# Four cross-attention and FFN layers: query projection by pairs of groups with a DMA spread, work moved to GpSimd, and a source order on two more engines

## The chip, the cores and the metric

The kernel runs on one core of a Trainium2 chip. The metric is the device time of one execution in microseconds. Before the change three runs gave a median of 4570.16 us (4563.57 to 4571.57). A separate profiled execution took 4577.85 us; the profile's span, from its first to its last instruction, is 4576.1 us. PE is the tensor engine, DVE the vector engine, ACT the scalar engine, POOL is GpSimd and SP the queue that issues most DMAs.

## The reference, cut to what matters

The input is `x` of 2048 rows by 256, a context of 1601 rows by 192 and a mask over the context. Four layers follow one another. Each adds a cross-attention of the normalised rows to the context, and then an FFN of the normalised rows.

```python
x = x + xattn(_layernorm(x), ctx)      # layers 0, 1, 3: 16 heads of 16; layer 2: 8 heads of 32
x = x + ffn(_layernorm(x))

# xattn
q, k, v = x @ wq + bq, ctx @ wk + bk, ctx @ wv + bv
scores = q k^T / sqrt(d)               # layer 3: masked context columns get -max
out = softmax(scores) v @ wo + bo

# ffn, with a router on the same normalised rows
# layer 0: sigmoid scores, 2 of 4 groups, then 4 of 16 experts, plus a shared MLP
# layer 1: 2 of 8 experts, gelu MLP of 1024;  layer 2: 2 of 8 linear experts
# layer 3: 2 of 16 experts with a capacity of 320 rows, plus a shared MLP and the row itself
```

Everything is computed in float32.

## The kernel before, in words

The rows are held in SBUF as four blocks of 512 rows (`x[b]`, each four tiles of 128 rows). The context is held transposed as `ctxT` (192 rows, and one further row of ones that carries the biases). Heads are worked on in four groups of 128 partitions: four heads in layers 0, 1, 3 (32 partitions for each, of which the head's 16 and two helpers are used), two in layer 2.

`load_attention` loads a layer's weights. It scatters the query weights on POOL into a padded copy `wq` of 512 columns, so that a projected group comes out already spread over its partitions. In layer 3 it also loads the mask as one row `mrow`. `keys_values` projects the keys in 16 tiles of about 400 columns, two matmuls each (lines 227 and 230), and in layer 3 a third matmul with one row of input (line 235) that writes the mask into a helper row of the keys. It then projects the values in 13 tiles.

`attention` then works in 16 steps, one for each block and group. A step has three parts.

- Maxima: `project_queries` (line 263, and the copy with bias and scale on ACT, line 267) makes `q1`. `max_unit` computes a score tile of 128 rows by 512 keys and reduces it to row maxima on DVE (lines 276, 283); `max_tails` does the last 65 keys (lines 292, 300). `max_rows` puts the maxima into a padded tile `mp`, and `with_maxima` transposes it and adds it to `q1` (lines 319, 320), so that the later exponential needs no subtraction.
- Scores: `score` computes transposed score tiles of 128 keys by 512 rows (line 328) and ACT takes the exponential (lines 336, 338).
- Values: `values` accumulates them over 13 key tiles (line 346). `copy_out` copies the accumulator (line 502), `normalise` transposes and divides (lines 358 to 362). After the four groups of a block, `outputs_T` and `project` add the projected output to `x[b]` (lines 374, 383, 391).

The order of this work is written out. `ORDER` lists one period of tokens, M for a maximum, S for a score, P for the values of a key tile; a step's maxima stand beside the scores and values of the step before it. Two slots make a period, and a step is 13 slots long. An agenda (`at(slot, ...)`) places the rest at slots: `points` are the slots two after the last maxima of a step. A query projection is placed two points ahead of its end in layers 0, 1, 3 (one in layer 2), the normalisation `rows(b)` for a block's queries four slots ahead of its transposes. After a block's output projection, `after(b)` gives the FFN's normalisation `rows`, its transposes `rows_T` and the router `route`. `norm_rows` (lines 398 to 406) takes the statistics, the power of -1/2 (on POOL, line 403) and the scaling on DVE, in one go.

In the loop's main part the tensor engine keeps this written order (`tc.manual_schedule` with `EngineType.PE`). On all other engines, and outside of that part, the framework's scheduler decides the order when the program is built. The first slots of a layer (its lead, maxima only) are issued in pieces between the FFN work of the layer before, and there too only PE's order is fixed. PSUM tiles come from one ring of seven banks, which maxima, scores, transposes and projections share; a bank comes free when DVE or ACT has read it.

Of the kernel before, what the change touches and what calls it, by code (L numbers as in the profile page):

```python
# [11 lines left out]
F32 = mybir.dt.float32  # L12
I32 = mybir.dt.int32
U32 = mybir.dt.uint32
U8 = mybir.dt.uint8
# [4 lines left out]
P = 128  # L20
# [4 lines left out]
NB = 4  # L25
# [41 lines left out]
def block_stack(ctx: ExitStack, tc: tile.TileContext, I: dict, out: bass.AP):  # L67
# [28 lines left out]
    nc.vector.memset(ctxT[DC - P : DC - P + 1, 1, :], 1.0)  # L96
    C1, C2 = P, DC - P + 1
# [24 lines left out]
    nc.vector.memset(neg_half, -0.5)  # L122

# [4 lines left out]
    nc.vector.tensor_scalar(mcol, mcol8, -1.0, BIG, ALU.add, ALU.mult)  # L128


    def load_attention(L):
# [3 lines left out]
        wq_raw = wp.tile([P, 2, D], F32, tag="wq_raw", name=f"wq_raw{n}")  # L135
        nc.sync.dma_start(wq_raw, I[f"wq{n}"])
        wq = wp.tile([P, 2, H * S], F32, tag="wq", name=f"wq{n}")
        nc.gpsimd.memset(wq, 0.0)
        wqv = wq.rearrange("p c (h s) -> p c h s", s=S)
        wqr = wq_raw.rearrange("p c (h e) -> p c h e", e=d)  # L140
        for g in range(NG):
            hs, up = slice(g * J, (g + 1) * J), L.up[g]
            nc.gpsimd.tensor_copy(wqv[:, :, hs, up : up + d], wqr[:, :, hs])
        W["q"] = wq
        kw = 2 * D if L.fused else D
        wk_raw = wp.tile([P, 2, kw], F32, tag="wk_raw", name=f"wk_raw{n}")
        nc.sync.dma_start(wk_raw[:, 0, :], I[f"wk{n}"][0:P, :])
        nc.sync.dma_start(wk_raw[0 : DC - P, 1, :], I[f"wk{n}"][P:DC, :])
        if L.biased:
            nc.sync.dma_start(wk_raw[DC - P : C2, 1, :], I[f"bk{n}"])  # L150
        else:
            nc.vector.memset(wk_raw[DC - P : C2, 1, :], 0.0)
# [3 lines left out]
        else:  # L156
            wv_raw = wp.tile([P, 2, D], F32, tag="wv_raw", name=f"wv_raw{n}")
            nc.sync.dma_start(wv_raw[:, 0, :], I[f"wv{n}"][0:P, :])
            nc.sync.dma_start(wv_raw[0 : DC - P, 1, :], I[f"wv{n}"][P:DC, :])
            if L.biased:  # L160
                nc.sync.dma_start(wv_raw[DC - P : C2, 1, :], I[f"bv{n}"])
            else:
                nc.vector.memset(wv_raw[DC - P : C2, 1, :], 0.0)
            k_src = wk_raw.rearrange("p c (h e) -> p c h e", e=d)
# [6 lines left out]
        nc.gpsimd.memset(wk[DC - P : C2, 1, :], -1.0)  # L171
        wkv = wk.rearrange("p c (h s) -> p c h s", s=S)
        for g in range(NG):
            hs, up = slice(g * J, (g + 1) * J), L.up[g]
            nc.gpsimd.tensor_copy(wkv[:, 0, hs, up : up + d], k_src[:, 0, hs])
            nc.gpsimd.tensor_copy(wkv[0:C2, 1, hs, up : up + d], k_src[0:C2, 1, hs])
        W["k"] = wk
        if L.masked:
            mk = wp.tile([1, J, S], F32, tag="mk", name=f"mk{n}")
            nc.vector.memset(mk, 0.0)  # L180
            nc.vector.memset(mk[:, :, d + 1 : d + 2], 1.0)
            mrow8 = wp.tile([1, M], U8, tag="wB", bufs=2, name="mrow8")
            nc.sync.dma_start(mrow8, I["mask_row"])
            mrow = wp.tile([1, M], F32, tag="wA", bufs=2, name="mrow")
            nc.vector.tensor_scalar(mrow, mrow8, -1.0, BIG, ALU.add, ALU.mult)
            W["mk"], W["mrow"] = mk, mrow
        bq = wp.tile([P, NG], F32, tag="bq", name=f"bq{n}")
        nc.vector.memset(bq, 0.0)
        if L.biased:
            for j in range(J):  # L190
                if J == 4:
                    nc.sync.dma_start(bq[j * S : j * S + d, :], I[f"bq{n}"][j])
                else:
                    for g in range(NG):
                        at = j * S + L.up[g]
                        nc.sync.dma_start(bq[at : at + d, g : g + 1], I[f"bq{n}"][j, :, g : g + 1])
        if L.masked:

            row = small.tile([P, 1], F32, tag="row", name="row")
            nc.vector.tensor_reduce(  # L200
                row, ident.rearrange("p (j s) -> p s j", s=S)[:, d + 1, :], AX.X, ALU.add
            )
            nc.vector.tensor_copy(bq, row.to_broadcast([P, NG]))
        else:
            nc.vector.tensor_scalar(bq, bq, L.scale, None, ALU.mult)
        W["bq"] = bq
# [11 lines left out]
    def keys_values(L, W):  # L218
# [4 lines left out]
        for g in range(NG):  # L223
            for lo, hi in zip(KEYB[:-1], KEYB[1:]):
# [7 lines left out]
                    start=False, stop=not L.masked,  # L232
                )
                if L.masked:
                    nc.tensor.matmul(
                        o, W["mk"].rearrange("o j s -> o (j s)"), W["mrow"][:, lo:hi], start=False, stop=True
                    )
# [21 lines left out]
    def project_queries(L, W, xnT, g):  # L259

        pq = ps_misc()
        for c in range(2):
            nc.tensor.matmul(  # L263
                pq, W["q"][:, c, g * P : (g + 1) * P], xnT[:, c, :], start=(c == 0), stop=(c == 1)
            )
        q1 = act.tile([P, BT], F32, tag="q", bufs=5, name="q1")
        nc.scalar.activation(q1, pq, AF.Identity, bias=W["bq"][:, g : g + 1], scale=L.scale)  # L267
        mx = small.tile([P, NT, L.J, len(KB) - 1], F32, tag="mx", name="mx")
        return q1, mx
# [34 lines left out]
    def max_rows(L, mx, g):  # L304

        d, S = L.d, L.S
        mp = act.tile([P, NT, P], F32, tag="mp", name="mp")
# [1215 lines left out]
```

## Time and profile before

| what | value |
|---|---|
| median of three runs | 4570.16 us (4563.57 to 4571.57) |
| profiled execution, its own time | 4577.85 us |
| span in its profile | 4576.1 us |
| mean granted PE clock | 0.952 |
| busy: PE, DVE, ACT, POOL | 4377.1, 2459.4, 1984.1, 436.9 us |
| maxima on DVE (line 283) | 2688 of 684 ns |
| exponentials on ACT (line 338, line 336 in layer 3) | 2080 of 599 ns, 832 of 686 ns |
| query projection on PE (line 263) | 256 records, 122.6 us |
| mask matmuls of layer 3 (line 235) | 32 records, 400-column ones 950 ns |
| scaling of the rows on DVE (line 406) | 128 of 406 ns |

The page cuts the span into 40 slices and gives each engine's busy share in tenths, and the granted clock of PE in tenths of full speed. Every float32 matmul appears as two records in the trace. A row of a group gives line, engine, operation, output and inputs, count, busy time, mean duration of one, and the idle time of the engine ahead of it with the engine that ended it. Matmuls overlap, so a group's mean is longer than the distance between two starts. A row of a timeline gives start, duration, engine, line, operation and count, and in brackets the idle time ahead of it and what ended it.

### The profile page before, as it was taken

What the parts mean: (1) busy time and instruction counts of PE and PEld (TensorE: products, weight loads), DVE (VectorE), ACT (ScalarE), POOL (GpSimd) and SP (SyncE); (2) the same over time, 40 slices, a digit from 0 to 9 for tenths busy, and PEclk for the clock granted to TensorE, in tenths of its full rate; (3) what the DMA queues carried; (4) which work ended last, traced back from release to release, by engine and by line L of the source; (5) the groups of instructions that cost most, each with busy time, mean ns of one, the idle gap of its engine ahead of it and who ended that gap; (6) DMA issues with size and microseconds to landing.
All of it is one profiled execution on the core that took longest, in us unless ns stands there. A gap on an engine that the chain in (4) does not pass through costs nothing. (4 is left out here: it accounts for less than half of the span.)

```text
span 4576.1 us, 62597 instructions
## 1 busy us (share of the span) xinstructions
PE 4377.1 (96%) x25260; PEld 2003.0 (44%) x25260; DVE 2459.4 (54%) x5215; ACT 1984.1 (43%) x3718; POOL 436.9 (10%) x515
## 2 busy tenths in 40 slices
PE   8999999999999999999997999999999999999795
PEld 5333333366643334336885333343443333333463
DVE  5666766424777666653223645441486667663222
ACT  1655655611156655563221344432016666665010
POOL 1000000000000000003444000000000000000323
PEclk8999999999999999999998899997799999999897
DMA  2000000000000000002542000000000000000054
GB/s 73 1 1 1 1 1 3 1 25 1 1 1 1 1 6 1 8 6 66 178 158 72 1 1 1 1 1 3 10 13 1 1 6 1 6 1 10 26 143 122
DMA packets 56952, 108.89 MB, mean 24 GB/s; under 512 B 16733, under 2 KB 38101, under 8 KB 52054
## 3 DMA queue, kind: packets, MB, share of 16 engines
q0 software_dynamic: 20864, 55.18, 4.2%
q1 hardware_dynamic: 35798, 49.71, 3.4%
q8 instruction: 199, 3.26, 0.3%
q14 instruction: 91, 0.75, 0.1%
HBM read 138.37 MB, written 16.88 MB: 34 GB/s over the span
## 5 line engine op out<-in xcount | busy, mean ns | idle before, releaser
L283 DVE TENSOR_REDUCE mx<-ps_m 128x1 f32<-128x512 f32 x2688 | 1701.0, 684 | 684.1 <-PE ps_m L276 398.5
L328 PE MATMUL ps_s<-q,kT 32*128 32x512 f32 (+2 forms) x5824 | 1741.1, 628 | 8.6 <-DVE mx L283 8.4
L276 PE MATMUL ps_m<-kT,q 32*128 32x512 f32 x5376 | 1601.8, 645 | 8.5 <-issue 6.0
L338 ACT ACTIVATE e<-ps_s 128x512 f32<-128x512 f32 (+1 forms) x2080 | 1112.3, 599 | 874.1 <-PE ps_s L328 685.6
L346 PE MATMUL ps_acc<-e,V 128*32 128x512 f32 (+2 forms) x5824 | 931.7, 612 | 5.7 <-ACT a L502 5.7
L328 PEld LDWEIGHTS ps_s<-q,kT 32*128 32x128 f32 (+2 forms) x5824 | 579.7, 182 | 691.9 <-DVE mx L283 406.9
L276 PEld LDWEIGHTS ps_m<-kT,q 32*128 32x128 f32 x5376 | 574.6, 188 | 487.8 <-issue 392.5
L336 ACT ACTIVATE e<-ps_s,mcol 128x512 f32<-128x512 f32 (+1 forms) x832 | 515.6, 686 | 238.0 <-PE ps_s L328 158.3
L346 PEld LDWEIGHTS ps_acc<-e,V 128*32 128x32 f32 (+2 forms) x5824 | 160.5, 112 | 644.0 <-issue 506.8
L309 POOL MEMSET mp<- 128x512 f32 x64 | 33.3, 527 | 2451.4 <-PE ps_m L319 2443.2
L1030 ACT ACTIVATE h<-ps_h,w 128x128 f32<-128x128 f32 x320 | 91.3, 369 | 218.1 <-issue 130.0
L267 ACT ACTIVATE q<-ps_m,bq 128x512 f32<-128x512 f32 x64 | 44.0, 688 | 295.4 <-PE ps_m L263 295.4
L809 DVE SCALAR_TENSOR_TENSOR x<-ps_m,cw,x 128x256 f32<-128x256 f32 x256 | 110.8, 479 | 92.6 <-PE ps_m L801 89.6
L1022 PE MATMUL ps_h<-xT,w 128*128 128x128 f32 x1280 | 152.7, 279 | 0.0
L772 ACT ACTIVATE h<-ps_h 128x512 f32<-128x512 f32 x80 | 47.7, 597 | 235.0 <-PE ps_h L771 235.0
L1022 PEld LDWEIGHTS ps_h<-xT,w 128*128 128x128 f32 x1280 | 149.4, 195 | 0.1
L300 DVE TENSOR_REDUCE mx<-ps_m 128x4 f32<-128x260 f32 x224 | 80.3, 422 | 126.0 <-PE ps_m L292 126.0
L1044 PE MATMUL ps_m<-w,h 128*128 128x256 f32 x640 | 144.6, 379 | 0.0
L361 DVE RECIPROCAL rec<-ps_m 128x16 f32<-128x16 f32 (+1 forms) x64 | 15.4, 240 | 206.9 <-PE ps_m L358 206.9
L1044 PEld LDWEIGHTS ps_m<-w,h 128*128 128x128 f32 x640 | 118.6, 190 | 14.5
L263 PE MATMUL ps_m<-xnT,wq 128*128 128x512 f32 x256 | 122.6, 610 | 0.2 <-ACT xnT L417 0.2
L1267 DVE TENSOR_TENSOR h<-ps_h,sg 128x320 f32<-128x320 f32 (+3 forms) x60 | 31.8, 530 | 167.5 <-PE ps_h L1260 123.0
(266 smaller groups left out, 3306.0 us busy)
## 6 DMA issues: line engine op xcount, KB each, us to landing
gu<-in_w_gate SPq DMA_DIRECT2D x16, 352.0 KB
gu<-in_w_up SPq DMA_DIRECT2D x16, 352.0 KB
ys_dram<-ys SPq DMA_DIRECT2D x40, 128.0 KB
xn_dram<-xn SPq DMA_DIRECT2D x8, 512.0 KB
dn<-in_w_down SPq DMA_DIRECT2D x16, 256.0 KB
ys<-ys_sb SPq DMA_DIRECT2D x32, 128.0 KB
x<-in_x SPq DMA_DIRECT2D x4, 512.0 KB
up<-in_expert_up SPq DMA_DIRECT2D x2, 1024.0 KB
```

The source lines that it names most:

```text
L263: nc.tensor.matmul(pq, W["q"][:, c, g * P : (g + 1) * P], xnT[:, c, :], start=(c == 0), stop=(c == 1))
L276: nc.tensor.matmul(pm, q1[at : at + 32, t * P : (t + 1) * P], kT[at : at + 32, g, KB[kb] : KB[kb + 1]], start=True, stop=True,)
L283: nc.vector.tensor_reduce(mx[:, t, j, kb : kb + 1], pm, AX.X, ALU.max)
L300: nc.vector.tensor_reduce(mx[:, :, j, 3:4], pm[:, 0 : NT * w].rearrange("p (t w) -> p t w", w=w), AX.X, ALU.max)
L328: nc.tensor.matmul(sp, kT[j * S : (j + 1) * S, g, c * P : c * P + cw], q2[j * S : (j + 1) * S, :], start=True, stop=True,)
L336: nc.scalar.activation(e[0:cw], sp, AF.Exp, bias=mcol[0:cw, c : c + 1])
L338: nc.scalar.activation(e[0:cw], sp, AF.Exp)
L346: nc.tensor.matmul(acc[j * S : (j + 1) * S, :], V[0:cw, c, h * (d + 1) : h * (d + 1) + S], es[j // 2][0:cw, j % 2, :], start=(c == 0), sto ...
L809: nc.vector.scalar_tensor_tensor(x[b][:, t, :], pd[:, i * D : (i + 1) * D], cws[b][:, t, e0 + e + i : e0 + e + i + 1], x[b][:, t, :], ALU. ...
L1022: nc.tensor.matmul(pu[:, (f - f0) * P : (f - f0 + 1) * P], w1[:, c * F1 + f * P : c * F1 + (f + 1) * P], xT[:, c, :], start=(c == 0), stop ...
L1030: nc.scalar.activation(h[:, f, :], pu[:, (f - f0) * P : (f - f0 + 1) * P], AF.Gelu, bias=w1[:, 2 * F1 + f : 2 * F1 + f + 1],)
L1044: nc.tensor.matmul(pd[:, 0:D], h[:, f, :], w2[:, f * D : (f + 1) * D], start=(f == 0), stop=(f == 7))
```

## The change

- Queries: the padded query weights go. `project_queries` projects 128 of the 256 query columns at once (eight heads of 16, or four of 32), so two projections serve a block in place of four. ACT copies the result to `qc`. `spread_queries` moves it by DMA on SP, one head at a time, to the group's tile `q1_tiles[i % 4]`, which was filled with zeros (layer 3: with the helper row of the mask) beforehand on POOL. It also clears `mp`, which `max_rows` did. `with_maxima` writes a new tile `q2`.
- Mask: `ctxT` gets a further row with the mask, computed once at the start and moved there by DMA. The third matmul of layer 3's keys goes, since a row of `wk` carries the helper row now. The second key matmul has 66 rows of input instead of 65.
- Normalisation: the statistics are cut into one call for each tile of 128 rows, at slots of their own; the addition of epsilon and the scaling move from DVE to POOL. After a block, the FFN's statistics are two slots apart, and the scaling, the transposes and the router follow later.
- Router: it becomes a generator with up to four stages, three slots apart. One-hot rows of all choices are made at once. The small arithmetic runs on POOL for the first three blocks and on DVE for the last; sums become halvings, and reciprocals on POOL become a power of -1. The copy of layer 1's logits moves to ACT.
- Order: in the main part DVE and ACT keep the source order too.
- The buffers `q` go from five to three; keys' and values' raw weights share one tile.

```diff
-            nc.gpsimd.tensor_copy(wqv[:, :, hs, up : up + d], wqr[:, :, hs])
+        wq = wp.tile([P, 2, D], F32, tag="wq", name=f"wq{n}")
+        nc.sync.dma_start(wq, I[f"wq{n}"])
...
+    nc.sync.dma_start(ctxT[CB:C2, 1, :], mrow)
...
-                if L.masked:
-                    nc.tensor.matmul(
-                        o, W["mk"].rearrange("o j s -> o (j s)"), W["mrow"][:, lo:hi], start=False, stop=True
-                    )
...
-                pq, W["q"][:, c, g * P : (g + 1) * P], xnT[:, c, :], start=(c == 0), stop=(c == 1)
+                pq, W["q"][:, c, m * P : (m + 1) * P], xnT[:, c, :], start=(c == 0), stop=(c == 1)
...
+    def spread_queries(L, qc, i, g):
+
+        q1 = q1_tiles[i % NG]
+        for j in range(L.J):
+            at, to = (g * L.J + j) * L.d % P, j * L.S + L.up[g]
+            nc.sync.dma_start(q1[to : to + L.d, :], qc[at : at + L.d, :])
+        mx = small.tile([P, NT, L.J, len(KB) - 1], F32, tag="mx", bufs=3, name="mx")
+        mp = act.tile([P, NT, P], F32, tag="mp", name="mp")
+        nc.gpsimd.memset(mp, 0.0)
...
-        nc.vector.tensor_tensor(q1, pt, q1, ALU.add)
-        return q1
+        q2 = act.tile([P, BT], F32, tag="q", bufs=3, name="q2")
+        nc.vector.tensor_tensor(q2, pt, q1, ALU.add)
+        return q2
...
+    def norm_rows(b, mv):
+
         rs = small.tile([P, NT], F32, tag="rs", name="rs")
-        nc.gpsimd.tensor_tensor(rs, ve, neg_half, ALU.pow)
+        nc.gpsimd.tensor_scalar(rs, mv[:, :, 1], LN_EPS, None, ALU.add)
+        nc.gpsimd.tensor_tensor(rs, rs, neg_half, ALU.pow)
...
-            nc.vector.tensor_scalar(
+            nc.gpsimd.tensor_scalar(
                 xn[:, t, :], x[b][:, t, :], mv[:, t, 0:1], rs[:, t : t + 1], ALU.subtract, ALU.mult
...
+    ORDERED = {mybir.EngineType.PE, mybir.EngineType.DVE, mybir.EngineType.Activation}
...
+                at_stats(r_slot - 8, b)
                 at(r_slot - 4, rows, b)
                 at(r_slot, rows_T, b)
...
-                at(slot + 1, a_rows)
-                slot = next_point(slot + 3)
+                for t in range(NT):
+                    at(slot + 2 + 2 * t, a_stats, t)
+                at(slot + 2 + 2 * NT, a_rows)
+                slot = next_point(slot + 4 + 2 * NT)
                 at(slot, a_rows_T)
-                at(next_point(slot + 1), a_route)
+                slot = next_point(slot + 1)
+                for k in range(STAGES):
+                    at(slot + 3 * k, next, a_route, None)
...
-        with tc.manual_schedule(engines={mybir.EngineType.PE}):
+        with tc.manual_schedule(engines=ORDERED):
             parts["main"]()
```

The router of layers 2 and 3 shows how the stages are cut (each `yield` ends one; `eng` is POOL or DVE):

```python
lg = tmp([NT, E], "r0")
nc.vector.tensor_tensor(lg, logits(xnT, wr, E), bc(br, NT), ALU.add)
mxr = tmp([NT, 1], "sm_m")
nc.vector.tensor_reduce(mxr, lg, AX.X, ALU.max)
e = tmp([NT, E], "r1")
eng.tensor_tensor(e, lg, mxr.to_broadcast([P, NT, E]), ALU.subtract)
nc.scalar.activation(e, e, AF.Exp)
yield
s = sum_columns(eng, e, E, "s")
over(eng, e, e, s)
yield
m8, i8f = top(e)
...
over(eng, w, m8[:, :, 0:2], s)
take(w, i8f)
```

## Prediction

> **What bounds the kernel now.** I read the page's busy shares and slices first, then the groups, then the stages by windows. TensorE (PE) is busy 96% of the span, VectorE (DVE) 54%, ScalarE (ACT) 43%, GpSimd (POOL) 10%.
>
> ```profile
> span 4576.1 us, 62597 instructions
> ...
> PE 4377.1 (96%) x25260; PEld 2003.0 (44%) x25260; DVE 2459.4 (54%) x5215; ACT 1984.1 (43%) x3718; POOL 436.9 (10%) x515
> ...
> PE   8999999999999999999997999999999999999795
> ...
> PEclk8999999999999999999998899997799999999897
> ...
> L263 PE MATMUL ps_m<-xnT,wq 128*128 128x512 f32 x256 | 122.6, 610 | 0.2 <-ACT xnT L417 0.2
> ```
>
> The PE row is 9 nearly everywhere, so work taken off PE's own queue is worth its full time, and work taken off DVE or ACT is worth only what PE waited for it. The clock row shows the second loss: where PE runs thin, its granted clock drops to a half. Four windows then: the key projections of layer 1 (before its first expert sums) and of layer 3; one plain attention step of layer 0 (copy of the accumulator, line 502, to the next copy); and the step with a block end in it.
>
> ```profile
> 932.40:958.40 26.00, 26.00 (x61) 14.01 (x60) 9.90 (x52) 3.95 (x8) 0.00 (x0) 0.78 0.01 1
> 3146.00:3217.30 71.30, 71.30 (x95) 26.23 (x95) 6.77 (x30) 3.95 (x8) 0.00 (x0) 0.50 0.00 0
> 350.40:399.40 49.00, 49.00 (x362) 18.24 (x362) 34.37 (x58) 30.26 (x57) 0.52 (x1) 1.00 0.00 1
> 399.40:457.80 58.40, 57.26 (x366) 21.57 (x370) 38.38 (x80) 29.52 (x55) 2.60 (x3) 0.94 0.00 1
> ```
>
> Columns: window, length, then busy (records) of PE, weight loads, DVE, ACT, POOL, and the granted clock. Layer 3 takes 71.3 us where layer 1 takes 26.0, and never leaves half clock. A plain step takes 49.0 us, the block-end step 58.4. The timeline inside the latter says why:
>
> ```profile
> 436.00 1.88 PE L263 MATMUL ps_m<-xnT,wq 128*128 128x512 f32 x4
> ...
> 437.72 3.62 PE L383 MATMUL ps_m<-wo,oT 128*128 128x256 f32 x16
> ...
> 440.38 0.75 DVE L398 BATCH_NORM_STATS2 st<-x 128x6 f32<-128x256 f32 x2
> ...
> 446.04 1.06 DVE L406 TENSOR_SCALAR xn<-x,mv,rs 128x256 f32<-128x256 f32 x3 [0.85 <-POOL rs L403]
> ...
> 447.75 1.07 PE L328 MATMUL ps_s<-q,kT 32*65 32x512 f32 x2 [1.14 <-DVE mx L283]
> ...
> 451.63 1.94 PE L346 MATMUL ps_acc<-e,V 128*32 128x512 f32 x8
> ```
>
> From 440 to 449 us DVE does the statistics of two blocks and a normalisation among the maxima that free PSUM. PE waits for a maximum; at 451.63 eight value matmuls take 1.94 us, which take 1.06 at full clock.
>
> **Part by part.** All sums are against the profiled execution (span 4576.1, its own time 4577.85, 7.7 above the median 4570.16).
>
> *(1) Query projection.* 64 projections (four PE records each) become 32; `q1` is then filled by 224 DMAs. PE price of one: 1.88 us busy with overlap at 436.00, 1.72 to the next operation's start. Like for like: in layer 0, copies 12 to 13, where the last projection is past, lie 47.3 us apart, against 49.0 for copies 4 to 5 and 8 to 9, with the same transposes: 1.7. I take 1.75, since some in the leads run at half clock: 32 x 1.75 = **-56** (-50 to -61, half of 122.6). ACT's 32 copies of 0.69 go too, worth nothing while ACT is at 43%.
>
> The DMAs are issued two points ahead in layers 0, 1, 3 (some 90 us) and one ahead in layer 2 (about 70 us), so the attention hides them; without that cover each step would show about 3 us. SP's order confirms the room: in the main loops loads behind a wait (`wq` of the next layer, `xn_dram` of a block) stand among spreads not needed for one or two points. The cover is missing at a layer's first step, which projects one slot before its first maximum:
>
> ```profile
> 2484.85 0.69 ACT L267 ACTIVATE q<-ps_m,bq 128x512 f32<-128x512 f32 x1 [1.87 <-PE ps_m L263]
> ...
> 2486.46 2.83 PE L276 MATMUL ps_m<-kT,q 32*128 32x512 f32 x14
> ```
>
> Today the maxima follow the copy's end by 0.9 us. A DMA needs 0.32 us on SP to issue and 1.6 to land (mask row: issued at 2455.49, consumer starts at 2457.06); four issues end 1.0 later. So 2 to 4 us at each of four starts, up to 3.4 more each if the gap halves the clock: take 3.3 each, **+13** (+8 to +27). Behind that first maximum PE's whole queue waits, FFN matmuls included.
>
> *(2) Mask as a context row.* Sixteen one-row matmuls (32 records) leave layer 3's keys. By their own group rows they cost about 27 us. But by the windows the stage falls from 71.3 towards 26.0: layer 1 does the same 15 remaining tiles and comes back to full clock after 12 us. Here the Trainium skill's "TensorE: Matmul & The Clock Gate" (Part 1) differs from the trace: it says about 3.4 us of sustained matmuls brings full clock. By it the removed work would be 32 x 0.34 = 11 us (0.34 is the warm pace of a 400-column key matmul, four in 1.35 us at 30.07); in the trace 71 us of back-to-back matmuls, a third of them one row high, stayed at 0.50, while layer 1's full-height ones recovered. That the low rows hold the clock down is an inference from these two stages. I take the rows: **-46**, between -31 (clock stays cold: 15 pairs x 2.67 = 40 us) and -51 (warm throughout). The context's extra row makes the other layers' keys 66 rows instead of 65: no columns more, so nothing.
>
> *(3) Normalisation off DVE, statistics spread.* DVE loses 128 x 0.41 = 52 us of scaling and 32 of the small adds; POOL gets them. What is worth anything is the block-end step. Its excess over a plain step is 9.4 us, of which the output projection, which stays, is 3.5. The same excess beyond 3.5 in all six such steps of layers 0, 1, 3: 5.8, 4.7, 5.7, 4.9, 7.1, 3.8 = 32 us (some 17 of it half clock); layer 2's show under 1 each. The new order puts one statistic after every eight maxima, and the scaling on POOL. I take three quarters, **-24** (-32 to 0).
>
> The price on POOL: no row has its two-scalar operation. Its copy of 128 elements takes 0.29, its two-input add of 1024 takes 2.35, so 256 elements lie between about 0.4 and 0.6; four make 1.8 against DVE's 1.38. In the main loop the transposes come four slots (14 us) later and hide it. At the four layer tails nothing does: +0.7 each, **+3** (0 to +8). The skill's "GPSIMD Engine Reference" (section 4.1) advises against elementwise work there, at about twice the time for two inputs, and "SBUF — State Buffer" (Who interferes with whom) has one of the two engines block fully while the other holds their common port, which DVE takes in two-port modes or with two SBUF inputs. If POOL's added 60-odd us of scaling stopped DVE, the maxima would slip and (3) would be nil or a loss of some 20. The row: from 65.92 to 68.25 POOL adds a bias block while 42 maxima take 25.18 us, 0.60 each, their usual pace. The maxima read PSUM; I keep the row.
>
> *(4) Routing staged and partly on POOL.* The routing steps of layers 0 and 3 exceed plain ones by 3.4 to 7.7 us, layer 1's by about 3; some 3.4 are logits and transposes that stay. So at most 9 us can come back. Against it, ACT, now in source order, holds the exponential of the router behind a POOL subtraction (9 blocks of layers 1 to 3), and the probability tiles of the attention wait behind it, then PE through PSUM: 1 us each. Net **0** (-8 to +10).
>
> *(5) Source order on DVE and ACT.* PE's order is unchanged but for the removed matmuls and later norm transposes and logits at block ends. In plain steps DVE and ACT already follow PE, so **0** (-10 to +15).
>
> *(6) Start and rest.* The mask row must be loaded (small loads of this stage land about 9 us after issue: `mcol` at 13.8), converted, and moved again by SP, with the key bias behind it. But query weights need no POOL work, and the first four key matmuls do not need the row: **+2** (-2 to +5). Tile `y` of the final gather gets three buffers for five; its gathers are issue-bound at 1.27 us, two per tile, so three tiles are 7.6 us against 6 to 7 from issue to use: **+1** (0 to +8).
>
> Sum: -56 +13 -46 -24 +3 +0 +0 +2 +1 = **-107**. Profile about 4470; median 4570 - 107 = **4463**.
>
> **Rivals.** *R1: removed matmuls count, relief doesn't.* DVE's bursts were not what stalled PE, or new in-order waits replace them; the leads cost double. -56 -46 +24 +8 = -70: 4500. For it: the project adds and divisions (2.7 us) still stand ahead of the maxima. Against: the wait at 447.75 names DVE, after the statistics. *R2: more than counted.* Keys warm at once (-51), all 32 us and 6 of routing return, leads cost 8: about -135: 4435. For it: clock drops are paid again by the wait that follows them. *R3, slower: spread DMAs land late in every step.* Place: SP's in-order queue, where a spread stands behind a load waiting for a tile to be free (`gu` of the last FFN, `wq`, `xn_dram`), and PE's maxima behind the spread. It decides from 107/64 = 1.7 us per step; at 3 us, the cover-less price, 64 steps cost 192 - 107 = +85: 4655. For it: one queue and 224 new entries. Against: points ahead as above. *R4: the clock stays cold in layer 3's keys*, -31 instead of -46: 4478; within the range.
>
> **How the numbers follow.** My forecast with R4, 4445 to 4485: 0.60; R1: 0.18; R2: 0.15; R3: 0.06; about no change: 0.01. The predicted time is the likeliest, 4463. The range for 8 in 10 reaches into R1 and R2, cutting the far half of each: 4430 to 4515. Faster by over 0.2% (9 us, about what a measurement of this kernel tells from no change) 0.93, within 0.01, slower 0.06.
>
> **What would show it.** Projection group 128 records, about 60 us; layer 3's keys in 26 to 32 us with a clock above 0.7; block-end steps near 53 us at clock 1.00; plain steps 47 and 49 in turn; 2 to 4 us before each layer's first maximum, named DMA. The prediction is wrong if PE shows DMA waits in the main loop, if ACT waits for POOL by tens of us, or if new half-clock stretches appear at the leads.

## The result, and the profile after

The changed kernel takes 4489.92 us (median of 4 runs, 4487.74 to 4502.23), beside 4566.86 for the kernel before in the same session (4 runs, 4559.13 to 4571.57). The ratio is 0.9839, with a 95% interval of 0.9815 to 0.9862: faster by 77 us. The profiled execution took 4487.74 us, 90 less than the profiled execution of before; the sums below are made between these two profiles, as the prediction's -107 was.

The page of the changed kernel, cut to the lines that answer to those shown of before (projection group: line 263 before, line 248 now; in each group row: count, busy time and mean ns, then PE's idle time just ahead of it and who ended it):

```profile
span 4486.0 us, 62975 instructions
...
PE 4258.6 (95%) x25100; PEld 1965.4 (44%) x25100; DVE 2414.3 (54%) x4911; ACT 1959.6 (44%) x3690; POOL 653.1 (15%) x833
...
PEclk8999999999999999999998799999899999999897
...
L277 PE MATMUL ps_m<-kT,q 32*128 32x512 f32 x5376 | 1604.8, 644 | 29.9 <-DMA q<-qc 18.5
...
L406 POOL TENSOR_SCALAR xn<-x,mv,rs 128x256 f32<-128x256 f32 x128 | 156.0, 1231 | 3.5
```

```profile
L248 PE MATMUL ps_m<-xnT,wq 128*128 128x512 f32 x128 | 64.2, 626 | 0.2 <-ACT xnT L417 0.2
```

(The second fence is from the full list of groups.) PE is 119 us less busy. Two things are new: the matmuls of the maxima wait for the DMA of a spread (18.5 us), and the scaling on POOL takes 1231 ns, three times DVE's 406.

The windows of the changed kernel answer to the four of before: keys of layer 1, keys of layer 3, a plain step of layer 0 (from one copy of the accumulator, now line 524, to the next), and the block-end step behind it. Columns are as before; the third number from the end is the granted clock.

```profile
903.00:931.00 28.00, 28.00 (x74) 16.11 (x74) 10.65 (x56) 5.43 (x10) 0.24 (x1) 0.79 0.01 1
3120.00:3148.10 28.10, 28.10 (x80) 16.80 (x81) 7.48 (x35) 4.18 (x9) 0.29 (x1) 0.82 0.01 1
345.40:394.40 49.00, 49.00 (x362) 18.23 (x362) 34.31 (x58) 30.27 (x57) 0.53 (x1) 1.00 0.03 7
394.40:445.00 50.60, 50.60 (x361) 19.62 (x364) 34.48 (x60) 28.63 (x54) 0.53 (x1) 1.00 0.00 1
```

Layer 3's keys now behave as layer 1's do: from the first key matmul to the first value matmul 28.0 us (3120.00 to 3148.04), at 0.82. Counted in the same way the stage took 76.5 before (3140.04 to 3216.53; the window of 71.3 us shown there begins one tile later), at 0.50. The block-end step is down from 58.4 to 50.6, at full clock; it has no projection now, which is 1.7 of the fall. The plain step shown keeps its projection, and its 49.0 us; every second one has lost it (in layer 0 48.8 to 47.1 and 49.6 to 47.9).

Between the first and the last accumulator copy of each layer, and in the stretches between layers (us; in brackets the time lost to half clock, that is half the length of the stretches in which the clock stood at 0.5):

| stretch | before | after | difference |
|---|---|---|---|
| start to layer 0 | 155.7 (17.1) | 154.2 (13.7) | -1.5 |
| layer 0 | 757.1 (13.7) | 729.9 (1.7) | -27.2 |
| 0 to 1 | 420.7 (11.9) | 425.5 (13.7) | +4.8 |
| layer 1 | 747.0 (8.5) | 726.6 (1.7) | -20.4 |
| 1 to 2 | 508.2 (47.8) | 516.5 (59.7) | +8.3 |
| **layer 2** | 539.1 (1.7) | 551.2 (15.4) | **+12.1** |
| 2 to 3 (holds layer 3's keys) | 331.4 (59.7) | 285.7 (25.6) | -45.7 |
| layer 3 | 751.5 (8.5) | 725.5 (0.0) | -26.0 |
| to the end | 365.5 (49.7) | 371.1 (51.7) | +5.6 |

Two things do not fit the prediction. Layer 2 lost six projections within its stretch (12 before, 6 now) and should have gained 10 us; it lost 12. And three of the four stretches behind a layer got longer by 5 to 8 us. A point of layer 2 shows the first, in the kernel before and then in the changed one:

```profile
2613.18 3.60 PE L263 MATMUL ps_m<-xnT,wq 128*128 128x512 f32 x8
...
2617.77 1.14 PE L276 MATMUL ps_m<-kT,q 32*128 32x512 f32 x8
...
2618.84 1.94 PE L346 MATMUL ps_acc<-e,V 128*64 128x512 f32 x8
```

```profile
2576.15 1.09 PE L315 MATMUL ps_m<-ident,mp 128*128 128x128 f32 x8
2577.08 1.88 PE L248 MATMUL ps_m<-xnT,wq 128*128 128x512 f32 x4
2578.89 1.12 PE L325 MATMUL ps_s<-q,kT 64*128 64x512 f32 x2
2579.72 2.41 SPq L263 DMA_DIRECT2D q<-qc  x4
2581.75 1.09 PE L277 MATMUL ps_m<-kT,q 32*128 32x512 f32 x2 [1.74 <-DMA q<-qc]
2583.06 2.62 PE L277 MATMUL ps_m<-kT,q 32*128 32x512 f32 x6 [0.21 <-DMA q<-qc]
2585.61 3.68 PE L343 MATMUL ps_acc<-e,V 128*64 128x512 f32 x8
```

The projection (2577.08) is followed by two score records and then at once by the maxima that need it. The four DMAs are issued at 2579.72, and PE stands for 1.74 us. The eight maxima records, 1.14 us in one run before, take 3.7 in two pieces. During the second the granted clock halves (2583.73 to 2590.56): eight value matmuls take 3.68 us, where they took 1.94. Four of layer 2's six points have such a half-clock stretch, 6.8 us each; the kernel before has none there. Their named waits are 0.2 to 2.0 us, and the maxima are drawn out at all four. At the other two points the output projection of a block stands between the projection and the maxima, and there is neither wait nor half clock.

The end of layer 2 shows the second, again before and then after:

```profile
3134.15 0.67 DVE L391 TENSOR_TENSOR x<-ps_m,x 128x512 f32<-128x512 f32 x1
...
3137.15 1.38 DVE L406 TENSOR_SCALAR xn<-x,mv,rs 128x256 f32<-128x256 f32 x4 [1.12 <-POOL rs L403]
...
3139.59 0.60 PE L594 MATMUL ps_m<-wr,xnT 128*128 128x8 f32 x2 [0.48 <-ACT xnT L417]
```

```profile
3110.18 0.67 DVE L388 TENSOR_TENSOR x<-ps_m,x 128x512 f32<-128x512 f32 x1
...
3112.04 0.23 POOL L402 TENSOR_SCALAR rs<-mv 128x4 f32<-128x4 f32 x1 [5.01 <-DVE mv L394]
3112.36 1.04 POOL L403 TENSOR_TENSOR rs<-rs,neg_half 128x4 f32<-128x4 f32 x1
3113.50 4.85 POOL L406 TENSOR_SCALAR xn<-x,mv,rs 128x256 f32<-128x256 f32 x4
3114.78 0.69 PE L416 MATMUL ps_m<-ident,xn 128*128 128x128 f32 x2 [4.75 <-POOL xn L406]
3115.99 0.69 PE L416 MATMUL ps_m<-ident,xn 128*128 128x128 f32 x2 [0.51 <-POOL xn L406]
...
3119.55 0.60 PE L621 MATMUL ps_m<-wr,xnT 128*128 128x8 f32 x2 [0.46 <-ACT xnT L417]
```

The transposes follow POOL's pace, 1.2 us a tile. From the last addition of the projection to the first logits it is 9.4 us (3110.18 to 3119.55); before, with DVE scaling, it was 5.4 (3134.15 to 3139.59).

### The profile page after: what moved, and what is told of

Read it like the earlier page. It is cut to its first block, busy times and chain, and to the rows that moved or that the text cites. A ratio compares the mean times of both kernels' runs of the same rounds, so it can differ in the third digit from the quotient of the medians.

```text
span 4486.0 us, 62975 instructions
## 1 busy us (share of the span) xinstructions
PE 4258.6 (95%) x25100; PEld 1965.4 (44%) x25100; DVE 2414.3 (54%) x4911; ACT 1959.6 (44%) x3690; POOL 653.1 (15%) x833
## 5 line engine op out<-in xcount | busy, mean ns | idle before, releaser
L325 PE MATMUL ps_s<-q,kT 32*128 32x512 f32 (+2 forms) x5824 | 1721.0, 623 | 0.7 <-DVE mx L284 0.6
L277 PE MATMUL ps_m<-kT,q 32*128 32x512 f32 x5376 | 1604.8, 644 | 29.9 <-DMA q<-qc 18.5
L406 POOL TENSOR_SCALAR xn<-x,mv,rs 128x256 f32<-128x256 f32 x128 | 156.0, 1231 | 3.5
L816 PE MATMUL ps_h<-xnT,up 128*128 128x512 f32 x256 | 117.9, 604 | 0.0
```

Of the source, the lines that this page charges most:

```text
L277: nc.tensor.matmul(pm, q1[at : at + 32, t * P : (t + 1) * P], kT[at : at + 32, g, KB[kb] : KB[kb + 1]], start=True, stop=True,)
L325: nc.tensor.matmul(sp, kT[j * S : (j + 1) * S, g, c * P : c * P + cw], q2[j * S : (j + 1) * S, :], start=True, stop=True,)
L406: nc.gpsimd.tensor_scalar(xn[:, t, :], x[b][:, t, :], mv[:, t, 0:1], rs[:, t : t + 1], ALU.subtract, ALU.mult)
L816: nc.tensor.matmul(pu, u(c), xnT[b][:, c, :], start=(c == 0), stop=(c == 1))
```

## The experiments

Each run is compared with the kernel before in its own session; ratios carry 95% intervals. The changed kernel itself is at 0.9839 [0.9815, 0.9862]. The kernel before had a median of 4554.83 to 4566.86 us, depending on the session, so two runs of different sessions are compared by their ratios and their profiles, not by their medians.

### Layer 2: projections four slots early

```diff
+            early = 4 if J == 2 and k >= 0 else 0
...
-            at(q_slot, begin_queries, i)
+            at(q_slot - early, begin_queries, i)     # projection and spread DMAs
+            at(q_slot, begin_maxima, i)              # mx and mp, as before
```

> The changed kernel, with layer 2's query projections and spread DMAs four slots (some 14 us) earlier; nothing else moves. Theory A: in layer 2 the first maximum follows its own projection at once, so PE waits about 2 us for the spread, and the half-clock stretch after it (4 times 3.4 us) is the wait's consequence. Then the waits of PE for a spread fall from 18.5 us to under 8, the four half-clock stretches of layer 2 are gone, and its stretch from first to last accumulator copy falls from 551 to about 527 us: 4466 in all. Rival B: the half-clock stretches come because a point now has one projection less of full-height work; then the waits go but the stretches stay, layer 2 takes about 541, and the time is about 4480.

Measured: 4471.27 us, ratio 0.9815 [0.9798, 0.9833]: 11 us better than the change by the ratio, within the intervals, and 13 by the profile. PE has no wait for a spread in layer 2, and the half-clock stretches at its points are gone (3.4 us lost in the layer for 15.4). So the clock fell as a consequence of the wait, as theory A has it; the missing projection is not the cause, since it is missing here too. The half clock does not follow every time: in the eight other profiles that leave layer 2's points as in the change, two or three of the four have it. There a step with the wait alone takes some 39 us and one with the full stretch 41.5 to 43.4, where this run has 36.5 to 38.3. But layer 2 took 536.9 us, not 527 (528.8 by six projections): a pair of steps gained 0.5 us over before where 1.7 were due, with no wait in the list of PE's waits. The timeline of this run shows where the rest is (line 329 is the score, 248 the projection, 281 the maximum):

```profile
2558.27 1.98 PE L329 MATMUL ps_s<-q,kT 64*128 64x512 f32 x6
2560.18 1.98 PE L248 MATMUL ps_m<-xnT,wq 128*128 128x512 f32 x4
2562.10 1.12 PE L329 MATMUL ps_s<-q,kT 64*128 64x512 f32 x2
...
2566.09 1.99 PE L329 MATMUL ps_s<-q,kT 64*128 64x512 f32 x8
```

These score matmuls have 64 rows of input, half of PE's rows, and two of them run side by side: eight records in one run (four matmuls, two records each) take 1.99 us. Parted into six and two they take 1.98 + 1.12, since the third and the fourth matmul each run alone. The four slots put the projection into the middle of such a group.

### Scaling back on VectorE, and the statistics at once

The first run changes `norm_rows` alone, the second the slots of the statistics alone.

```diff
-            nc.gpsimd.tensor_scalar(
+            nc.vector.tensor_scalar(
                 xn[:, t, :], x[b][:, t, :], mv[:, t, 0:1], rs[:, t : t + 1], ALU.subtract, ALU.mult
```

> The changed kernel, with the scaling of the normalisation back on VectorE (4 x 0.41 us a block in place of 4 x 1.23 on GpSimd). Theory S: what relieved the block ends is the spreading of the statistics, so block-end steps stay at 50.5 to 51 us, and each of the four layer tails gets back about 3.9 us: 4474. Rival D: the scaling on VectorE was what stalled the block ends; then these steps return to 54 to 58 us (6 of them, +20 to +45), and the time is 4495 to 4520.

```diff
-                at(slot + t, stats, t)
+                at(slot + NT - 1, stats, t)
...
-                    at(slot + 2 + 2 * t, a_stats, t)
+                    at(slot + 2, a_stats, t)
```

> The changed kernel, with the four statistics of a block in one slot again instead of one in every second slot (or every slot, in layer ends ahead of a projection); the scaling stays on GpSimd. Theory S (spreading did it): the block-end steps go from 50.5 to 54 us or more, with a half-clock stretch in most, and the time is about 4490 + 6 x 5 = 4520. Rival D (the scaling's removal did it): the steps stay under 52, the time within 5 us of 4490.

Measured: scaling on DVE 4462.23 us, 0.9795 [0.9779, 0.9812], 20 us better than the change by the ratio and 25 by the profile; statistics at once 4503.07, 0.9892 [0.9875, 0.9909]. In **both** the block-end steps stay at 50.5 to 51.1 us. With scaling on DVE the stretches between layers fall by 2.5 (0 to 1), 12.0 (1 to 2) and 3.5 (to the end); between layers 2 and 3 nothing is gained, and layer 2 has two half-clock stretches fewer. With the statistics at once (its profile is 7 us longer than the change's, its ratio 0.0053 higher), only the steps in which the next block's input is normalised grow, by 1.6 us each. So neither the scaling alone nor the bunching alone stalls the block ends: both of the expected theories, as far as they named one cause, are refuted.

### The burst: both undone, in two places, and parted

```diff
 # all with the scaling on nc.vector; statistics of the input in one slot too
-                    at(slot + 2 + 2 * t, a_stats, t)
-                at(slot + 2 + 2 * NT, a_rows)
+                    at(slot + 1, a_stats, t)      # late burst: slot + 10; parted: slot + 1
+                at(slot + 1, a_rows)              # late burst: slot + 10; parted: slot + 5
```

> The changed kernel, with both halves of the normalisation's change undone: all four statistics of a block, GpSimd's power and the scaling on VectorE in one burst, one slot after the output projection, as in the kernel before; VectorE and ScalarE stay in source order. Theory P (place and burst together stalled the block ends; taking either half of it away was enough): the block-end steps of layers 0, 1 and 3 go back from 50.5 to 55 us or more, most with a half-clock stretch, and the time is 25 to 45 above the run with scaling on VectorE alone (4462), about 4495. Rival O: the written order of VectorE is what relieved them; then they stay under 52 us and the time is within 8 us of 4462.

> The same burst (four statistics, power, scaling on VectorE, all in one slot), but nine slots later, where the change has its scaling. Theory P: the place decides, as the projection's adds and divisions and the next block's normalisation are past by then; block-end steps under 52 us, the time near 4462. Rival B: the burst itself decides, wherever it stands; then the steps are 55 us or more here too, and the time about 4495.

> As the burst on VectorE (statistics of all four tiles in one slot, one slot after the output projection; scaling on VectorE), but the scaling stands four slots (some 14 us) behind the statistics instead of behind them in the same slot, for both normalisations. VectorE does the same work in the same neighbourhood; what goes is its in-order wait for GpSimd's power (1.47 us of 5.0 in the burst) and the joining of the two runs of instructions. Theory W (a stretch without maxima of some 5 us is more than PSUM's seven buffers cover, one of 2 us is not): block-end steps under 52 us and no half clock there, layers 0 and 1 at 730 to 740 us, the time about 4470. Rival V (so much work of VectorE near the block end costs its time wherever it is parted): steps of 54 us or more, the time above 4510.

Measured:

| run | median, ratio | layer 0 (half-clock loss) | block-end steps of layer 0 | largest other step of layer 0 |
|---|---|---|---|---|
| scaling on DVE, statistics spread | 4462.23, 0.9795 | 729.8 (1.7) | 50.5, 50.5 | 52.9 |
| burst | 4573.04, 1.0044 [1.0029, 1.0060] | 757.3 (18.8) | 56.8, 56.8 | 55.7 |
| late burst | 4557.74, 1.0005 [0.9995, 1.0014] | 753.8 (15.4) | 50.5, 50.5 | 59.4 |
| parted by four slots | 4489.03, 0.9836 [0.9814, 0.9857] | 732.1 (1.7) | 52.1, 52.1 | 50.9 |

The burst eats the whole gain of the change: about 100 us between its profile and that of DVE scaling alone, far more than the 25 to 45 expected. It keeps DVE in source order, which the kernel before did not, so this is not the price of the block ends before (32 us of excess in the prediction's count); no run has the burst with DVE's order left to the scheduler. Moved nine slots on, it stalls there as badly (55.1 and 59.4 us in the steps behind the block ends), so the place is not the cause: theory P falls by 95 us, and rival B, nearer, is still 62 short. Parted by four slots, the same instructions in the same neighbourhood cost one or two microseconds a step and no half clock there. The expected 4470 was 19 too low by the medians; 9 of these are the session, whose kernel before was that much slower. Against the run with DVE scaling the profile is 27 longer: 15 in layers 0, 1 and 3, and 8 in the stretch from layer 1 to 2. Of the 15, 5 lie in the last routing steps of layers 1 and 3, with a half-clock stretch that in layer 1 begins just behind the router's matmuls of 8 columns; what brings it there is not shown. The timeline of the burst at the first block end of layer 0:

```profile
447.36 0.42 DVE L393 BATCH_NORM_STATS2 st<-x 128x6 f32<-128x256 f32 x1
...
449.39 0.18 DVE L394 BATCH_NORM_AGGREGATE mv<-st 128x2 f32<-128x6 f32 x1
...
449.67 0.23 POOL L402 TENSOR_SCALAR rs<-mv 128x4 f32<-128x4 f32 x1 [10.22 <-DVE mv L394]
449.98 1.04 POOL L403 TENSOR_TENSOR rs<-rs,neg_half 128x4 f32<-128x4 f32 x1
451.05 1.38 DVE L406 TENSOR_SCALAR xn<-x,mv,rs 128x256 f32<-128x256 f32 x4 [1.47 <-POOL rs L403]
452.34 3.08 DVE L284 TENSOR_REDUCE mx<-ps_m 128x1 f32<-128x512 f32 x5
...
453.08 1.16 PE L277 MATMUL ps_m<-kT,q 32*128 32x512 f32 x2 [2.41 <-DVE mx L284]
...
456.88 1.94 PE L343 MATMUL ps_acc<-e,V 65*32 65x512 f32 x8
```

From 447.36 to 452.34 DVE takes no maximum: 2.2 us of statistics, 1.47 of waiting in order for POOL's power, 1.3 of scaling. PE runs out of free PSUM tiles and stands 2.41 us, and at 456.88 eight value matmuls take 1.94 us instead of 1.06: the wait is paid a second time in half clock. In the run with scaling on DVE a stretch of statistics between maxima is 0.6 us and the power is long done when the scaling comes. A 5 us stretch costs 4 to 9 us a place; one of about 2 us costs 1.6 at the block ends.

### Source order, and the engine of the routing

```diff
-    ORDERED = {mybir.EngineType.PE, mybir.EngineType.DVE, mybir.EngineType.Activation}
+    ORDERED = {mybir.EngineType.PE}
```

> The changed kernel, with only TensorE in source order in the main loops, VectorE and ScalarE ordered by the scheduler again. Theory of the prediction: in the plain steps the order is the same and the time stays within 10 us of 4490. Rival O: the written order is what keeps the spread statistics among the maxima; without it they bunch, the block-end steps return to 55 or more, and the time is 4515 or more.

Measured: 4516.5 us, 0.9916 [0.9899, 0.9932]; its profile is 14 us longer than that of the change. The plain steps are the same to 0.1 us, as the prediction had it. The block-end steps rise by 1 once a layer (51.6, in layer 3 52.1), not to 55. What comes back is the routing: 55.6 and 52.8 us in layer 0, 55.7 and 55.1 in layer 3 (49.8, 48.9; 50.2, 49.3 in the change), with a half-clock stretch in each. In DVE's timeline of such a step all the stages of a routing stand within 537.4 and 544.3, with three maxima among them; in the change the first stage takes 0.9 us, and three maxima follow 0.5 later. So the scheduler undoes the stages when it is free to, and the written order is worth more than the nothing that the prediction gave it: between 14 us (profiles) and about 35 (ratios; the profiled execution, 4501.39, was the fastest of its four by 15 us).

```diff
-            eng = nc.vector if b == NB - 1 else nc.gpsimd
+            eng = nc.vector
```

> The changed kernel, with the routing of all blocks on VectorE, staged as in the change (its elementwise steps leave GpSimd). Theory: the staging matters, not the engine; the route steps stay at 49 to 50 us and the time within 5 us of 4490. Rival: VectorE has no room among its maxima; the route steps go back to 52 to 56 us (5 of them or more), and the time to 4505 or more.

Measured: 4499.2 us, 0.9853 [0.9828, 0.9877], by the ratio not clearly apart from the change, by the profile 12 longer. The route steps proper do stay at 49.8 and 48.9; two steps of layer 0 behind them rise to 56.2 and 54.2, with half clock, and two of layer 3 by 1.6. Both theories are half right: the staging keeps the first steps clean, and behind them DVE has no room for layer 0's arithmetic. Which of its instructions stall there is not shown.

### The mask alone, and a tall mask

The first is the kernel before with the context row and nothing else. The second is the kernel before with its third matmul made 128 rows high, 127 of them zeros.

```diff
-                if L.masked:
-                    nc.tensor.matmul(
-                        o, W["mk"].rearrange("o j s -> o (j s)"), W["mrow"][:, lo:hi], start=False, stop=True
-                    )
```

> The kernel before, with the mask as a context row and nothing else of the change: 32 one-row matmul records leave layer 3's keys. Theory: the one-row matmuls held the clock at a half; without them the stage falls from 71 to about 28 us and the time by 43 to 46, to 4522. Rival (the removed records at a warm pace, 0.34 us each): the stage was cold for another reason and stays cold for 40 us or more; a fall of 11 to 31, 4536 to 4556.

```diff
-            mk = wp.tile([1, J, S], F32, tag="mk", name=f"mk{n}")
+            mk = wp.tile([P, J, S], F32, tag="mk", name=f"mk{n}")
...
-            mrow = wp.tile([1, M], F32, tag="wA", bufs=2, name="mrow")
+            mrow = wp.tile([P, M], F32, tag="wA", bufs=2, name="mrow")
+            nc.vector.memset(mrow, 0.0)
```

> The kernel before, with the mask still in a third matmul of each key tile, but 128 rows high (127 of them zeros) instead of one row: as many records, as many columns. Theory: the low rows hold the clock down; then layer 3's keys come back to full clock after some 12 us and take about 28 + 32 x 0.34 = 39 us in place of 71, the time is about 4535. Rival: the number of records or the third write to the group matters, not the height; then the stage stays at half clock for 71 us and the time at 4567.

Measured: context row alone 4519.71 us, 0.9897 [0.9873, 0.9920], that is -47 by the ratio; keys in 27.6 us (3147.29 to 3174.91), for 76.5. Tall mask 4530.99 us, 0.9925 [0.9902, 0.9949], that is -34; keys of layer 3 in 38.9 us (3129.16 to 3168.02; as many records as before). The end of the stage in the kernel before (247 is the first value matmul), and the start of it in the tall run (228 and 231 are the two key matmuls, 236 the mask):

```profile
3213.44 1.54 PE L230 MATMUL ps_m<-ctxT,wk 65*128 65x400 f32 x2
3214.91 1.70 PE L235 MATMUL ps_m<-mrow,mk 1*128 1x400 f32 x2
3216.53 1.22 PE L247 MATMUL ps_m<-wv_raw,ctxT 128*128 128x256 f32 x2
```

```profile
3136.30 1.54 PE L228 MATMUL ps_m<-ctxT,wk 128*128 128x400 f32 x2
3137.63 1.54 PE L231 MATMUL ps_m<-ctxT,wk 65*128 65x400 f32 x2
3138.97 0.94 PE L236 MATMUL ps_m<-mrow,mk 128*128 128x400 f32 x2
3139.74 0.83 PE L228 MATMUL ps_m<-ctxT,wk 128*128 128x400 f32 x2
```

The same 32 extra records, 128 rows high, let the clock rise after 10 us; one row high they held it at a half for the whole stage. In the kernel before it rose at 3220.73, 4.2 us after the values had taken over from the one-row matmuls. That the height decides is shown, not only argued: nothing else differs but the rows of zeros.

### Scaling on VectorE only where the transposes follow at once

```diff
-            xn[b] = norm_rows(b, mvs.pop(b))
+            xn[b] = norm_rows(b, mvs.pop(b), nc.vector if b == 0 else nc.gpsimd)
...
-                kept[b] = norm_rows(b, kept[b])
+                kept[b] = norm_rows(b, kept[b], nc.vector if b == NB - 1 else nc.gpsimd)
```

> The changed kernel, with the scaling on VectorE for the last block of each layer's output normalisation and for the first block of each layer's input normalisation, on GpSimd for the others. Theory: GpSimd's 1.23 us an operation is paid only where the transposes follow at once: the last block, four times about 3.9 us, so 4474; the block-end steps are not touched. Rival: the tail's time comes back in the wait behind it (weights, context keys), and the time stays within 5 us of 4490.

Measured: 4459.38 us, 0.9768 [0.9742, 0.9794], twice the expected gain. In the profile, 28 us shorter, the stretch from layer 1 to 2 gives 16.0, start and 0 to 1 give 3.1 and 3.3, layer 2 4.4 (half clock lost fell by 5.2 there, though its points are as in the change), 2 to 3 only 1.3 and the end 0.2. So the four tails at 3.9 us each are not what came back. The windows of that stretch, first the changed kernel, then this run:

```profile
2036.10:2552.60 516.50, 451.79 (x2564) 358.37 (x2564) 178.64 (x535) 121.73 (x380) 221.00 (x231) 0.88 0.35 108
```

```profile
2028.40:2528.90 500.50, 443.92 (x2564) 355.15 (x2564) 181.00 (x543) 121.45 (x379) 211.12 (x223) 0.91 0.35 112
```

There POOL is also the engine that issues the gathers of layer 1's expert output. In the changed kernel it scales layer 2's first block from 2437.37 to 2442.21, adds a bias, and issues the next gather only at 2444.82, 11.5 us after the one before it ended; here that pause is 7.9 us. PE stands for about as long in both runs ahead of the transposes (21.9 us there, 20.9 here). The rest of the 16 us is half clock: 59.7 us are lost to it there and 46.1 here, and the mean clock of the stretch is 0.88 and 0.91 (0.91 before). How much of that the scaling causes is not settled by one profile of each: over all the changed kernel's variants the stretch takes 511.9 to 516.5 us with POOL's scaling at this place and 496.4 to 513.0 with DVE's, on average 11 apart. The prediction priced the tails and not this place.

### Both repairs

```diff
+            early = 5 if J == 2 and k >= 0 else 0
 # and the scaling as in the run above
```

> The changed kernel, with the scaling on VectorE for the first block of each layer's input and the last of its output normalisation, and layer 2's projections five slots early in place of none (five, not four: at four the projection parts a group of row-tiled score matmuls into six and two). Theory: the DMA waits and half-clock stretches of layer 2 are gone and no group is parted by the earlier place; layer 2 takes 527 to 531 us, where four slots early took 537, and the time is 4459 - 18 = 4441. Rival: the parted group is not what cost the 8 us; then layer 2 takes 537 again and the time is 4449.

Measured: 4442.1 us (4438.04 to 4446.39), 0.9752 [0.9739, 0.9766]; by the difference in ratio some 40 us faster than the change. Against the scaling alone (0.9768) the timed ratio gives only 7 us, within the intervals, and that the median meets the expected 4441 is in part luck: the kernel before measured beside it was 10 us faster than the one beside the scaling alone. What the earlier projections gave is read from the profiles. Layer 2 takes 530.7 us, for the 528.8 due. Its timeline shows the projection between whole groups, and the spread issued 15 us before the maxima that read it, which begin at 2559.92:

```profile
2541.38 1.14 PE L281 MATMUL ps_m<-kT,q 32*128 32x512 f32 x8
2542.45 1.98 PE L248 MATMUL ps_m<-xnT,wq 128*128 128x512 f32 x4
2544.37 1.94 PE L347 MATMUL ps_acc<-e,V 128*64 128x512 f32 x8
2545.19 2.41 SPq L263 DMA_DIRECT2D q<-qc  x4
2546.24 1.99 PE L329 MATMUL ps_s<-q,kT 64*128 64x512 f32 x8
```

The odd steps of layer 2 fell by 1.0 us against the run with four slots (37.4 to 36.4): the parted group is what cost most of the missing time there. In the profile 13.4 us were gained over the scaling alone, not 18; a half-clock stretch in layer 0 gave 3.0 back.

## Why the prediction came out as it did

The predicted 4463 was 27 us too low and the measured 4490 lies within 4430 to 4515. The total alone would have spoken for R1 (4500, removed matmuls count and relief doesn't); the profile does not: the relief came in full, and other terms were lost. That the total still came this near is in part luck: some 22 us lost in layer 2 and what POOL's pace cost were not in the sum, and 8 more at the block ends and 5 in the routing, which needed the source order, were not either.

- **(1) Query projection, -56 predicted.** Right: the group is 128 records and 64.2 us, and plain steps fall by 1.72. Of the leads' +13 the waits for a spread in all four starts are 3.0, 3.0, 5.5 and 2.9 us, 14.4 in all. The step that failed is "one ahead in layer 2 (about 70 us), so the attention hides them". In that layer one point ahead of a pair's *end* is exactly its *beginning*; 70 us is the distance to the last maximum; the first stands one pair of score records (1.1 us) behind the projection. This cost 22 us: 551.2 for the 528.8 that six projections less would give. Of these 13.7 are half clock and 4.1 named waits for the DMA; the rest is not named by a row, but lies where the maxima go in two pieces. R3 had named the mechanism, but for the wrong place: not a load in SP's queue, but no cover at all.
- **(2) Mask, -46.** Right in mechanism and size: -48 in the stage, -45.7 in the stretch around it, -47 alone; the clock is 0.82, for the 0.7 asked for. R4 is refuted. Here the row was the better guide. The Trainium skill's "TensorE: Matmul & The Clock Gate" (Part 1) has full clock after about 3.4 us of sustained matmuls; in the key stages of layers 1 and 3 it came 9 to 17 us after the first key matmul, and with one-row matmuls among them not in 76, though behind those, in the value matmuls, it came after 4.2.
- **(3) Relief of the block ends, -24.** Better than that: all six steps together fell by 42.6 us, of which 6 x 1.72 are the projection that no longer stands there, so 32.3, the whole excess. The reason given, bursts on DVE, holds: with both halves undone the steps take 56.3 to 57.0 us. The two halves of the change are not worth a share each, but either is enough alone.
- **(3) POOL's scaling, +3.** The mechanism was right, the size wrong: the step "256 elements lie between about 0.4 and 0.6" took a copy and an add as neighbours of a two-scalar operation, which measured 1.23. The tail of layer 2 takes 3.9 us longer, not 0.7 (the prediction's own 1.8 and 1.38 are 0.4 apart), and at layer 2's start the scaling stands among the gathers. The run with scaling on DVE at these places got back 28 us in the profile, most of them there and not at the tails. The warning of "GPSIMD Engine Reference" (section 4.1) against elementwise work there was set aside for the wrong reason: the port it was weighed with did not matter (the maxima on DVE took 685 ns, 684 before), the pace did. The same row of that page has one-input operations roughly at line rate; this one, with two per-partition scalars, measured three times VectorE's time.
- **(4) Routing, 0 within -8 to +10.** The route steps gave 15 us (25.6 less six projections), and the steps behind them, in layers 0 and 1, took back 10: -5.
- **(5) Source order, 0 within -10 to +15.** Outside its range: without it the kernel is slower by 14 us in the profile, and by more in the ratio. The plain steps are the same, as said; but (4) only holds with it.
- **(6) Start and the final gather, +3.** The start is 1.5 faster; the stretch to the end is 5.6 longer. With the tail's scaling on DVE one run got back 3.5 of it and another 0.2, so the cause of most of it stays open.

Of what was to show the prediction wrong, PE's DMA waits came true in the main loop of layer 2. ACT's waits for POOL did not: 15 us in all, not tens. Half clock at the leads grew in one stretch, that from layer 1 to 2, from 47.8 to 59.7 us lost. Not on the list was PE's wait for the scaling: 49.6 us for POOL's, 35.6 for DVE's before (the longest single wait, 21.9 and 21.2, is in both the one behind layer 1's expert sums).

What stays open: which of its instructions make layer 0's routing on DVE stall, how much of the stretch between layers 1 and 2 is due to POOL's scaling, and why the stretch to the end is longer. The gain in timed medians (77) is smaller than that between the two profiles (90), as the profile of before lies 11 us above the median of its session and that of after 2 below; the parts above are of the 90.

## What to carry to other kernels

A distance in time is the distance to the *first* consumer: list the stream between a producer and the first instruction that reads it, for each layer's own order, before a DMA is called hidden. An engine that feeds PSUM back to PE has a longest stretch that it may be away; here 2 us were cheap and 5 were expensive, so two small relief measures were worth no more than one, and a chain through another engine inside that stretch counted as being away. And work moved to a slower engine is free only where nothing waits for it: at the edges of a loop the old engine can keep it.

## What the runs showed of the hardware

- One-row matmuls hold the granted clock down: 32 records of them among 64 of 128 and 65 rows kept 76 us of unbroken PE work at 0.50; with 128 rows, zeros included, the clock was full after 10 us, and the stage took 38.9 us, though it had as many records.
- Where layer 2's maxima stood behind their spread (named waits of 0.2 to 2.0 us, eight records drawn out from 1.14 to some 3.6 to 4.0 us), 6.8 us at half clock followed in most cases, 3.4 us lost: more than the wait itself. With the spread earlier there was none at these places.
- On POOL the two-scalar operation on 128 x 256 float32 takes 1.23 us (DVE: 0.41), though a two-input addition of four times the elements takes 2.35: one operation's time could not be scaled from another's by element count.
- Matmuls of 64 rows run two at a time: eight records in 1.99 us. A group parted by another matmul takes 1.98 + 1.12.
